# A two-layer graph network on one core: first routing spread over ScalarE and POOL, joined waves, slot operand in pieces, own room for first gathers

## The chip, the cores and the metric

The kernel runs on one core of a Trainium2 chip. The metric is the device time of one execution in microseconds; lower is better. The core has five engines that work side by side: TensorE (PE, with its weight loads as PEld), VectorE (DVE), ScalarE (ACT), GpSimd (POOL) and SyncE (SP), which here only issues DMA transfers. ScalarE and POOL issue transfers too.

## The reference

1250 nodes with 1024 features pass through two layers. Each layer adds a graph convolution and a linear attention to the rows, and then a mixture of experts. The change sits in the first layer's graph convolution and expert routing, and in the second layer's first steps:

```python
# L0_gnn: norm = dinv[src] * dinv[dst];  h = x @ W
out = segment_sum(h[src] * norm[:, None], dst) + b
x = x + relu(out) + L0_mix(xn)
# L0_ffn on layernorm(x), T = 1250, E = 8, K = 2
cap = int(1.25 * ((T * K + E - 1) // E))             # 391
probs = softmax(x @ router_gate)
topw, topi = top_k(probs, 2); topw = topw / (topw.sum(-1) + 1e-9)
gates[t, topi] = topw
top_g, tok_idx = top_k(gates.T, cap)                 # each expert keeps its 391 best tokens
xe = x[tok_idx]
h = silu(xe @ gate_w) * (xe @ up_w)
out.at[tok_idx].add((h @ down_w) * top_g)
# L1: x = x + sage(xn) + mix(xn), then x = x + ffn(layernorm(x))
```

## The kernel before

The rows are cut into ten tiles of up to 128 (`TS`, `TOK`). Work is written tile by tile; the framework that builds the kernel orders each engine's instructions at build time by its own estimate of when each is ready, so that an engine's order need not be that of the code. Each engine then works its list strictly in order. Tiles of memory come from pools with a fixed number of buffers; all PSUM results share eight banks (`bank`).

The first routing is one loop over tiles. In step `t`:

- the rows are loaded as `xt` (three buffers) in two halves on SP's queue (L691, L692);
- `gcn_rows` (L540) sums the neighbours into `pg` with 20 products (10 source tiles, each with a high and a low part; L497), scales and adds the bias on VectorE (`rgcn`, L544), and adds the relu to `xt` on VectorE (L546). The sum goes back to `res_d` (L694);
- `normalise` calls `layernorm` (L132): statistics on VectorE (L136, L138), the root on ScalarE (L140), the reciprocal and the final `(x - mean) * rs` on VectorE (L142, L143). The result `xn` is stored to `x1n_d` from ScalarE's queue (L598);
- `logits` of tile `t - 1` transposes `xn` (`pt`, eight 128x128 pieces, L607), copies it out as `xnt` with `evac` (which takes ScalarE and VectorE in turn, L115 and L117), and multiplies by the router (`plg`, 16 products, L612); `lg` is copied by VectorE (L613);
- at the end of a wave of tiles, `choose` takes the softmax (Exp on ScalarE, L621), the two best experts and their weights, some 22 small VectorE instructions.

Before, the waves are `[(0, 4), (4, 8), (8, 9), (9, 10)]`. One step after a wave is chosen, `turn_over` transposes its gates and choices (`ptg`, L646), and `rank` counts for every token how many tokens of its expert have a larger gate: a product `prow` (L666) brings the gates of a wave beside the tokens of a tile, and VectorE counts from PSUM (`junk`, L656 and L659). There are 80 such products over the four waves.

After the loop the counts are summed (`above`, L715), and places become a table of token numbers: `at_slot` (128x2560, one VectorE instruction, L727), `hit` and `what` (L730, L733), and 20 products `ptab` (L737), then `idx` and `idx_q`. For the first expert four indirect gathers on POOL (L775) bring rows into `xe`, which has two buffers; TensorE transposes them (`pte`, L781). Later experts gather quarters of rows into `xq` (L787). Each expert then runs `pgate`, `pup` (L809) and `py` (L821), some 63 us, and stores to `y_d` (L826).

The second layer begins with ten tiles of: load rows (`xt`, L877), gather two expert results (`yt`, L883, POOL), add them (L886), store, normalise, transpose, multiply. Ahead of it POOL clears `projT` and `kv` (L839, L843).

Of the kernel before, what the change touches and what calls it, by code (L numbers as in the profile page):

```python
# [10 lines left out]
F32 = mybir.dt.float32  # L11
F32R = mybir.dt.float32r
# [10 lines left out]
P = 128  # L23
# [3 lines left out]
T = 10  # L27
# [19 lines left out]
WAVES = [(0, 4), (4, 8), (8, 9), (9, 10)]  # L47
# [54 lines left out]
def network(tc: tile.TileContext, a: dict, out: bass.AP, env: SimpleNamespace, exact: bool):  # L102
# [29 lines left out]
    def layernorm(dst, x, ts):  # L132
# [9 lines left out]
        nc.vector.reciprocal(rs[:ts], sd[:ts])  # L142
        return nc.vector.tensor_scalar(dst, x, mv[:ts, 0:1], rs[:ts], op0=OP.subtract, op1=OP.mult)  # L143
# [396 lines left out]
    def gcn_rows(t, hn, b, x):  # L540
# [5 lines left out]
        nc.vector.scalar_tensor_tensor(x, r[:TS[t]], 0.0, x, op0=OP.max, op1=OP.add)  # L546
# [13 lines left out]
    with tc.tile_pool(name="route0a", bufs=1) as ra, tc.tile_pool(name="route0w", bufs=2) as rw:  # L560
# [31 lines left out]
        counted = {}  # L592

        def normalise(t, xt):
            ts = TS[t]
            xn = rw.tile([P, D], F32, name="xn1")
            layernorm(xn[:ts], xt[:ts], ts)
            nc.scalar.dma_start(x1n_d[TOK[t], :], xn[:ts])  # L598
            return xn

        def logits(t, xn):
            ts = TS[t]
            xnt = rw.tile([P, KB, P], F32, name="xnt")
            for b0 in (0, 4):
# [4 lines left out]
                evac(xnt[:, b0:b0 + 4, :ts], pt.rearrange("p (b q) -> p b q", b=4)[:, :, :ts])  # L609
# [3 lines left out]
            nc.vector.tensor_copy(lg[:ts, t, :], pl[:ts, :E])  # L613
# [27 lines left out]
        def turn_over(t0, t1):  # L641
            n = sum(TS[t0:t1])
            for src, dst in ((g2, gT), (oh2[:, 0], ohT[:, 0]), (oh2[:, 1], ohT[:, 1])):
# [3 lines left out]
                evac(dst[:, t0 * P:t0 * P + n], pt[:40, :n])  # L647
# [38 lines left out]

        ready, chosen = [], []
        for t in range(T + 1):
            if t < T:
# [3 lines left out]
                gcn_rows(t, hn, b, xt[:TS[t], 512:])  # L693
                nc.sync.dma_start(env.res_d[1][TOK[t], 512:], xt[:TS[t], 512:])  # L694
                ready.append(normalise(t, xt))
            if chosen:
                turn_over(*WAVES[chosen[0]])
                rank(chosen.pop())
            if t:
                logits(t - 1, ready[t - 1])  # L700
                for wave, (t0, t1) in enumerate(WAVES):
                    if t1 == t:
                        choose(t0, t1)
                        chosen.append(wave)
        turn_over(*WAVES[chosen[0]])
        rank(chosen.pop())
# [13 lines left out]
        for j in range(2, NG):  # L720
# [5 lines left out]
        at = tb.tile([P, T, 2, P], F32R, name="at_slot")  # L726
        nc.vector.tensor_tensor(at, slots.unsqueeze(1).unsqueeze(1).to_broadcast([P, T, 2, P]),  # L727
                                place.unsqueeze(3).to_broadcast([P, T, 2, P]), op=OP.is_equal)
# [4 lines left out]
        nc.vector.tensor_mul(what, hit, token.unsqueeze(3).to_broadcast([P, T, 2, E * NG]))  # L733
        pt = bank("ptab")
        for t in range(T):
            for k in range(2):
# [22 lines left out]
    s_table.close()  # L759
    loops(OP.subtract)  # L760
# [4 lines left out]
    with s_route:  # L765
        quarters = x1n_d.rearrange("n (j f) -> (n j) f", j=4)
        with tc.tile_pool(name="moe0", bufs=2) as mp:
            def columns(e):
                xeT = mp.tile([P, KB, ROWS], F32, name="xeT")
                if e == 0:  # L770

                    for g in range(NG):
                        n = min(P, SLOTS - g * P)
                        xe = mp.tile([P, D], F32, name="xe", bufs=2)
# [57 lines left out]

    s_x1 = ExitStack()
# [501 lines left out]
```

## Time and profile before

| | us |
|---|---|
| median of 3 runs | 3562.47 (3558.68 to 3562.52) |
| the profiled execution | 3579.93 |
| its span | 3578.2 |
| TensorE busy | 3381.7 |
| VectorE busy | 939.7 |
| POOL busy | 581.2 |
| ScalarE busy | 281.5 |
| mean granted TensorE clock | 0.966 |

The span runs from the first to the last instruction of one profiled execution. Busy time is summed by engine; TensorE's matmuls are pipelined, so that its busy time is no measure of work at full speed. PEclk is the share of full clock that TensorE was granted. A wait `A <- B: total, times, longest` says that A's engine was idle until B was done. In the timeline a row has start, duration, engine, line, operation, result and operands, and in brackets the idle time of the engine before it.

### The profile page before, as it was taken

What the parts mean: (1) busy time and instruction counts of PE and PEld (TensorE: products, weight loads), DVE (VectorE), ACT (ScalarE), POOL (GpSimd) and SP (SyncE); (2) the same over time, 40 slices, a digit from 0 to 9 for tenths busy, and PEclk for the clock granted to TensorE, in tenths of its full rate; (3) what the DMA queues carried; (4) which work ended last, traced back from release to release, by engine and by line L of the source; (5) the groups of instructions that cost most, each with busy time, mean ns of one, the idle gap of its engine ahead of it and who ended that gap; (6) DMA issues with size and microseconds to landing.
All of it is one profiled execution on the core that took longest, in us unless ns stands there. A gap on an engine that the chain in (4) does not pass through costs nothing.

```text
span 3578.2 us, 30558 instructions
## 1 busy us (share of the span) xinstructions
PE 3381.7 (95%) x12418; PEld 2119.7 (59%) x12418; DVE 939.7 (26%) x2482; ACT 281.5 (8%) x580; POOL 581.2 (16%) x493
## 2 busy tenths in 40 slices
PE   7999999999997689999789999999999999988997
PEld 3474756644655456767535465547777554557775
DVE  4257345621225512322160000011111111241111
ACT  1000011100001000000001011100000000001111
POOL 0016775051000231200020000010000000012221
PEclk9999999999998589999889999999999999988999
DMA  4724221062222143433460100120000110228884
GB/s 148 169 67 111 25 24 1 24 220 99 75 83 86 55 135 132 165 119 137 134 234 27 47 24 24 56 102 35 24 24 24 36 59 28 89 73 286 273 259 100
DMA packets 165010, 342.75 MB, mean 96 GB/s; under 512 B 37468, under 2 KB 58883, under 8 KB 162685
## 3 DMA queue, kind: packets, MB, share of 16 engines
q1 hardware_dynamic: 100204, 242.14, 20.0%
q0 software_dynamic: 39616, 52.68, 7.4%
q10 hardware_dynamic: 25040, 45.89, 3.8%
q8 instruction: 100, 1.64, 0.2%
q14 instruction: 50, 0.40, 0.0%
HBM read 261.79 MB, written 78.87 MB: 95 GB/s over the span
## 4 chain that ended last, share of the span: by engine, by line
PE 88%; DVE 5%; DMA 4%; issue 2%; ACT 1%; POOL 0%; SPq 0%; ACTq 0%; POOLq 0%; DVEq 0%
PE ph L158 8%; PE ppn L158 8%; PE pwo L158 8%; PE pqT L855 8%; PE pv L158 6%; PE pqk L158 6%; PE p L1265 5%; PE pa L497 5%; PE pgate L809 5%; PE pup L809 5%; PE py L821 5%; PE ph L996 4%; PE py L1276 2%; PE pg L497 2%; PE pkv L351 2%; PE po L399 2%
## 5 line engine op out<-in xcount | busy, mean ns | idle before, releaser
L259 POOL DMA_INDIRECT adj_d<-cnt,cell x167 | 259.3, 1552 | 90.0 <-issue 42.8
L1265 PE MATMUL p<-xeT,w 128*128 128x256 f32 (+1 forms) x1088 | 192.8, 338 | 4.8 <-ACT xeT L115 4.3
L809 PE MATMUL pgate<-xeT,wg 128*128 128x392 f32 x512 | 178.5, 500 | 10.6 <-issue 10.6
L1265 PEld LDWEIGHTS p<-xeT,w 128*128 128x128 f32 x1088 | 171.4, 191 | 24.8 <-ACT xeT L115 7.9
L809 PE MATMUL pup<-xeT,wu 128*128 128x392 f32 x512 | 176.3, 496 | 6.6 <-issue 6.6
L821 PE MATMUL py<-hT,wd 128*128 128x392 f32 x512 | 169.8, 492 | 0.0
L182 POOL TENSOR_TENSOR xr<-xr,bo 128x512 f32<-128x512 f32 (+1 forms) x40 | 50.4, 1264 | 714.3 <-PE pwo L158 453.8
L821 PEld LDWEIGHTS py<-hT,wd 128*128 128x128 f32 x512 | 160.5, 314 | 9.0
L158 PE MATMUL pqk<-wk,x0T 128*128 128x512 f32 (+1 forms) x320 | 145.3, 608 | 8.9 <-ACT x0T L115 7.5
L158 PE MATMUL pv<-wv,x1T 128*128 128x512 f32 (+1 forms) x320 | 144.2, 608 | 5.7 <-DVE x1T L117 3.4
L809 PEld LDWEIGHTS pgate<-xeT,wg 128*128 128x128 f32 x512 | 98.6, 193 | 82.7 <-issue 14.3
L809 PEld LDWEIGHTS pup<-xeT,wu 128*128 128x128 f32 x512 | 98.0, 191 | 81.2 <-issue 11.0
L158 PE MATMUL ph<-ws,h1T 128*128 128x512 f32 (+1 forms) x320 | 143.2, 596 | 0.0
L158 PE MATMUL pqk<-wq,x0T 128*128 128x512 f32 (+1 forms) x320 | 140.7, 593 | 0.0
L158 PE MATMUL ppn<-wn,x1T 128*128 128x256 f32 (+1 forms) x640 | 138.8, 379 | 0.0
L996 PE MATMUL ph<-x1T,ws 128*128 128x416 f32 (+1 forms) x384 | 138.2, 512 | 0.0
L158 PE MATMUL pv<-wv,x0T 128*128 128x512 f32 (+1 forms) x320 | 138.0, 592 | 0.0
L158 PE MATMUL ph<-wgcn,x0T 128*128 128x512 f32 (+1 forms) x320 | 138.0, 593 | 0.0
L158 PE MATMUL pwo<-wo,attn0T 128*128 128x512 f32 (+1 forms) x320 | 137.7, 592 | 0.1
L158 PE MATMUL ppn<-wn,h1T 128*128 128x512 f32 (+1 forms) x320 | 137.7, 592 | 0.0
L158 PE MATMUL pwo<-wo,attn1T 128*128 128x512 f32 (+1 forms) x320 | 137.5, 592 | 0.0
L855 PE MATMUL pqT<-x1T,wk 128*128 128x416 f32 (+1 forms) x384 | 135.6, 512 | 0.0
(369 smaller groups left out, 4460.2 us busy)
## 6 DMA issues: line engine op xcount, KB each, us to landing
w<-in_L_ffn_w_dram SPq DMA_DIRECT2D x17, 2048.0 KB
w<-in_L_ffn_w_dram SPq DMA_DIRECT2D x17, 1024.0 KB
wg<-in_L_ffn_gate_w_dram SPq DMA_DIRECT2D x8, 2048.0 KB
wu<-in_L_ffn_up_w_dram SPq DMA_DIRECT2D x8, 2048.0 KB
wd<-in_L_ffn_down_w_dram SPq DMA_DIRECT2D x8, 2048.0 KB
y_d<-ye ACTq DMA_DIRECT2D x30, 416.0 KB
adj_d<-ezero SPq DMA_DIRECT2D x2, 6105.0 KB
res_d<-xr SPq DMA_DIRECT2D x45, 256.0 KB
```

What stands on the lines that cost most here:

```text
L158: nc.tensor.matmul(pr[:TS[t], :cols], xT[:, k, TOK[t]], w[:, k, :], start=(k == 0), stop=(k == nk - 1))
L182: nc.gpsimd.tensor_add(xr[:TS[t]], xr[:TS[t]], bias[:TS[t]])
L259: nc.gpsimd.indirect_dma_start(out=adj_d[e % 2], out_offset=bass.IndirectOffsetOnAxis(ap=cell[:, e:e + 1], axis=0), in_=cnt[:, e:e + 1], i ...
L351: nc.tensor.matmul(pkv[f][:, :65], kf[:TS[t], i, f * P:(f + 1) * P], v[:TS[t], t, h, :], start=(t == 0), stop=(t == T - 1))
L399: nc.tensor.matmul(po[:TS[t], i, :], qf[:, hh, f, i * P:i * P + TS[t]], kv[:, h, f, :], start=(f == 0), stop=(f == 1))
L497: nc.tensor.matmul(pa, edges if by_node else feats, feats if by_node else edges, start=(s == 0 and i == 0), stop=(s == T - 1 and i == len( ...
L809: nc.tensor.matmul(pw[:, :SLOTS], w[:, k, ic], xeT[:, k, :SLOTS], start=(k == 0), stop=(k == KB - 1))
L821: nc.tensor.matmul(py[:, :SLOTS], wd[:, i, b::KB], hT[:, i, :], start=(i == 0), stop=(i == I0 // P - 1))
L855: nc.tensor.matmul(pq[:, :n], w[:, k, pair * P:(pair + 1) * P], xT[:, k, c0:c0 + n], start=(k == 0), stop=(k == KB - 1))
L996: nc.tensor.matmul(ps[:, :n], w[:, k, q0 + f * P:q0 + (f + 1) * P], xT[:, k, c0:c0 + n], start=(k == 0), stop=(k == KB - 1))
L1265: nc.tensor.matmul(pw_[:, :n], w12[:, k, off + i * P:off + (i + 1) * P], xeT[:, k, :n], start=(k == 0), stop=(k == KB - 1))
L1276: nc.tensor.matmul(py, hT[:, i, c * P:(c + 1) * P], w3[:, i, half * 512:(half + 1) * 512], start=(i == 0), stop=(i == H1 // P - 1))
```

## The change

It edits the routing loop, the table, the first expert's gathers and the placing of several pools:

- the last two waves become one, `(8, 10)`; `prow` products become 60;
- `rank` of a wave runs two tiles after its choice, behind the `logits` of that step;
- for all tiles but the last, the relu goes to ScalarE and the add to POOL (`gcn_rows`), and the last step of `layernorm` becomes two ScalarE passes and one small VectorE instruction;
- `xnt`, `lg` and the turned tables are copied by ScalarE alone; `x1n_d` is stored from SP's queue; an Exp on one column is placed behind the last norm;
- `at_slot` is made in five pieces of two tiles, after `hit` and `what`, between the `ptab` products;
- the first expert's four gathers have room of their own, in the two `xq` buffers;
- the second layer's `xt` rows get a pool of their own that is opened before the experts, its two clears move from POOL to VectorE, and `route1`, `pick1`, `x1T` and `h1T` are placed elsewhere (with `gw` loaded and `sc`, `so_far` cleared ahead of the second layer).

```diff
-WAVES = [(0, 4), (4, 8), (8, 9), (9, 10)]
+WAVES = [(0, 4), (4, 8), (8, 10)]
...
-    def layernorm(dst, x, ts):
+    def layernorm(dst, x, ts, last_on_act=False):
...
+        if last_on_act:
+            mm = small.tile([P, 1], F32, name="mm")
+            nc.vector.tensor_scalar(mm[:ts], mv[:ts, 0:1], -1.0, None, op0=OP.mult)
+            nc.scalar.activation(dst, x, AF.Identity, bias=mm[:ts])
+            return nc.scalar.activation(dst, dst, AF.Copy, scale=rs[:ts])
         return nc.vector.tensor_scalar(dst, x, mv[:ts, 0:1], rs[:ts], op0=OP.subtract, op1=OP.mult)
...
-    def gcn_rows(t, hn, b, x):
+    def gcn_rows(t, hn, b, x, spread=False):
...
-        nc.vector.scalar_tensor_tensor(x, r[:TS[t]], 0.0, x, op0=OP.max, op1=OP.add)
+        if spread:
+            nc.scalar.activation(r[:TS[t]], r[:TS[t]], AF.Relu)
+            nc.gpsimd.tensor_add(x, r[:TS[t]], x)
+        else:
+            nc.vector.scalar_tensor_tensor(x, r[:TS[t]], 0.0, x, op0=OP.max, op1=OP.add)
...
-            layernorm(xn[:ts], xt[:ts], ts)
-            nc.scalar.dma_start(x1n_d[TOK[t], :], xn[:ts])
+            layernorm(xn[:ts], xt[:ts], ts, last_on_act=t < T - 1)
+            if t == T - 1:
+
+                tc.keep_in_program_order(nc.scalar.activation(power, eps_t, AF.Exp))
+            nc.sync.dma_start(x1n_d[TOK[t], :], xn[:ts])
...
-                evac(xnt[:, b0:b0 + 4, :ts], pt.rearrange("p (b q) -> p b q", b=4)[:, :, :ts])
+                nc.scalar.copy(xnt[:, b0:b0 + 4, :ts], pt.rearrange("p (b q) -> p b q", b=4)[:, :, :ts])
...
-            nc.vector.tensor_copy(lg[:ts, t, :], pl[:ts, :E])
+            nc.scalar.copy(lg[:ts, t, :], pl[:ts, :E])
...
-                evac(dst[:, t0 * P:t0 * P + n], pt[:40, :n])
+                nc.scalar.copy(dst[:, t0 * P:t0 * P + n], pt[:40, :n])
...
-        for t in range(T + 1):
+        for t in range(T + 2):
...
-                gcn_rows(t, hn, b, xt[:TS[t], 512:])
+                gcn_rows(t, hn, b, xt[:TS[t], 512:], spread=t < T - 1)
...
-            if chosen:
-                turn_over(*WAVES[chosen[0]])
-                rank(chosen.pop())
-            if t:
+            if 0 < t <= T:
                 logits(t - 1, ready[t - 1])
...
-                        chosen.append(wave)
-        turn_over(*WAVES[chosen[0]])
-        rank(chosen.pop())
+                        chosen.append((wave, t))
+            while chosen and (chosen[0][1] < t - 1 or t == T + 1):
+                wave = chosen.pop(0)[0]
+                turn_over(*WAVES[wave])
+                rank(wave)
...
-        at = tb.tile([P, T, 2, P], F32R, name="at_slot")
-        nc.vector.tensor_tensor(at, slots.unsqueeze(1).unsqueeze(1).to_broadcast([P, T, 2, P]),
-                                place.unsqueeze(3).to_broadcast([P, T, 2, P]), op=OP.is_equal)
...
+        at = tb.tile([P, T, 2, P], F32R, name="at_slot")
         pt = bank("ptab")
         for t in range(T):
+            if t % 2 == 0:
+                nc.vector.tensor_tensor(at[:, t:t + 2], slots.unsqueeze(1).unsqueeze(1).to_broadcast([P, 2, 2, P]),
+                                        place[:, t:t + 2].unsqueeze(3).to_broadcast([P, 2, 2, P]), op=OP.is_equal)
...
     s_table.close()
+
+    s_rows = ExitStack()
+    rows1 = s_rows.enter_context(tc.tile_pool(name="rows1", bufs=3, side="right"))
     loops(OP.subtract)
...
+                    room = [mp.tile([P, NI, B, KB], F32, name="xq").rearrange("p i c b -> p (i c b)") for _ in range(2)]
...
-                        xe = mp.tile([P, D], F32, name="xe", bufs=2)
+                        xe = room[g // 3][:, g % 3 * D:(g % 3 + 1) * D]
...
-    xT = s_x1.enter_context(tc.tile_pool(name="x1T", bufs=1, side="right")).tile([P, KB, N], F32, name="x1T")
+    xT = s_x1.enter_context(tc.tile_pool(name="x1T", bufs=1)).tile([P, KB, N], F32, name="x1T")
...
-        nc.gpsimd.memset(projT, 0.0)
+        nc.vector.memset(projT, 0.0)
...
-        nc.gpsimd.memset(kv, 0.0)
+        nc.vector.memset(kv, 0.0)
...
-                    lnp = s_ln.enter_context(tc.tile_pool(name="ln1", bufs=3))
+                    lnp = s_ln.enter_context(tc.tile_pool(name="ln1", bufs=2))
...
-                        xt = lnp.tile([P, D], F32, name="xt2")
+                        xt = rows1.tile([P, D], F32, name="xt2")
...
-                            yt = lnp.tile([P, D], F32, name=f"yt{k}", bufs=2)
+                            yt = lnp.tile([P, D], F32, name=f"yt{k}")
...
-    h1T = s_sage.enter_context(tc.tile_pool(name="h1T", bufs=1)).tile([P, KB, N], F32, name="h1T")
+    h1T = s_sage.enter_context(tc.tile_pool(name="h1T", bufs=1, side="right")).tile([P, KB, N], F32, name="h1T")
```

The allocations of `route1` and `pick1`, with the `gw` load and the clears of `sc` and `so_far`, move unchanged from behind the second layer's attention to ahead of `x1T`.

## The prediction

> **What bounds the kernel now.** I read the page's busy shares first, then the chain of waits to find where TensorE is not on it, then the stages there by windows, waits and timeline.
>
> ```profile
> PE 3381.7 (95%) x12418; PEld 2119.7 (59%) x12418; DVE 939.7 (26%) x2482; ACT 281.5 (8%) x580; POOL 581.2 (16%) x493
> ```
>
> TensorE bounds the kernel as a whole, so only stretches where it idles can be won. The change touches two: the first routing (1042 to 1236.5 us) and the hand-over from the first experts to the second layer (1766.9 to 1799.1).
>
> ```profile
> core 0: us, PE busy (x) PEld busy (x) DVE busy (x) ACT busy (x) POOL busy (x), PEclk, DMA share, GB/s
> 1062.00:1087.00 25.00, 23.89 (x138) 19.99 (x137) 13.71 (x30) 3.79 (x7) 1.29 (x3) 1.00 0.49 170
> 1087.00:1112.00 25.00, 10.67 (x47) 8.29 (x47) 17.21 (x84) 3.68 (x7) 0.68 (x4) 0.72 0.25 91
> 1145.10:1205.30 60.20, 39.95 (x139) 28.50 (x138) 50.07 (x256) 5.68 (x11) 2.79 (x14) 0.56 0.03 11
> 1205.30:1236.50 31.20, 12.37 (x57) 10.96 (x57) 11.42 (x26) 2.08 (x5) 13.44 (x14) 0.55 0.35 106
> 1766.90:1799.10 32.20, 0.00 (x0) 0.00 (x0) 7.28 (x12) 1.78 (x3) 7.66 (x8) 0.55 0.72 232
> ```
>
> See the four kinds: a TensorE-bound tile loop; a hole at the first wave; a tail where VectorE (50 of 60 us) sets the pace at half clock; and two stretches where table, gathers and loads follow each other. Two waits name the hole:
>
> ```profile
> PE ptg L646 <- DVE g L636: 19.2, 4, 7.7
> PE plg L612 <- DVE xnt L117: 12.5, 6, 6.3
> ```
>
> **The loop and the hole (gain 8).** The loop's period is 8.0 us (rgcn at 1063.4, 1071.3, 1079.4): pg 20 x 0.23 = 4.7, pt 1.04, plg 1.95, small gaps. From the end of pg of tile 5 (1087.0) to the start of tile 6's (1111.1) are 24.1 us, of which TensorE's own work (12 ptg at 0.24, 8 prow at 0.28, pt and plg 3.0) is 8.2: 15.9 us are wait. First for the choice (ptg 7.7), then because the xnt copy sits on VectorE behind 8.4 us of counts (6.3) and tile 6's pg behind that plg. The change ranks wave 0 two tiles later, when the choice is long done, and copies xnt, lg and the turned tables on ScalarE. What is late next: 8 prow products want the 8 PSUM banks, freed at about 1 us each by the counts; and the choice still swaps ScalarE's table twice (1.28 each) ahead of one norm (ACT_TABLE_LOAD, 1283 ns). I leave 4 us of wait, between 0 and 8: 12 saved.
>
> Against it stands a longer chain to xn. It loses the 0.69 (L546) and the 0.81 (L143) on VectorE and gets a relu on ScalarE, an add on POOL, a small VectorE instruction (0.16) and two ScalarE passes of 1024. The groups have the nearest rows:
>
> ```profile
> L182 POOL TENSOR_TENSOR xr<-xr,bo 128x512 f32<-128x512 f32 (+1 forms) x40 | 50.4, 1264 | 714.3 <-PE pwo L158 453.8
> ...
> L278 ACT ACTIVATE sq<-q 128x512 f32<-128x512 f32 x36 | 22.7, 631 | 117.4 <-DVE q L276 102.5 <-DVE dup L252 8.8 <-DVE off L256 3.2
> ```
>
> Relu 0.63 and add 1.26 for 0.69; two passes of 1.07 (0.63 plus 512 more elements at (0.597 - 0.272)/384 = 0.85 ns, from L908's kf of 512 and 128) for 0.81: with the small one and four hand-overs of 0.05, about 3 us more per tile for tiles 0 to 8. VectorE gives back 2.4 us of queue per tile (0.69, 0.81, the 0.68 xnt copy, the 0.17 lg). Before, the chain from pg to xn took 6.6 us (1063.2 to 1069.9) and pt came 1.2 us later; bare it would be 3.8, so 2.8 were queueing. So it becomes 6.8 to 9.6, against the 7.7 to 8.0 that TensorE has of other work: mostly covered. If that cover is gone, the cost is up to 1.6 us x 8 tiles = 13.
>
> The GPSIMD Engine Reference of the Trainium skill (4.1 Engine selection) speaks against this: elementwise work belongs on VectorE, GpSimd being about 2x slower with two inputs. The rows agree on the price (1264 against 691 ns). By the rule the swap loses (0.63 + 1.26 - 0.69) x 9 = 11 us and the total falls to 24; by the rows most lies under the next pg, and the rule says nothing of that. I follow the rows. The skill's SBUF page (Who interferes with whom) adds that a VectorE and a GpSimd instruction can lock each other out; no row here shows it (POOL's adj, L489, takes 0.41 to 0.46 beside a busy VectorE). Bounds: 0 to one 0.75 instruction a tile, 7 us; I take 0 and keep 7 for the range.
>
> Both xnt copies in one queue also run plg in one piece. Before, tiles 6 to 8 did so, and their pg ran part of its way at 0.43 instead of 0.23 us a product (6.3 against 4.9 us): a period of 9.7. I charge 1 us to each of four tiles: 4. Net 12 - 4 = 8, between -5 and 14. The x1n_d stores move from ScalarE's queue to SP's: ten issues of 0.35 us. Each waits there for its Copy, and behind it queue the next res_d store and the xt loads, for which an add three tiles on waits. Those loads need the same tile's buffer back and have two periods (16 us) to land, which took 3.5 to 5.4 in the chain: 0, and 3 if that cover goes.
>
> **The tail (gain 15).** From the end of the last pg (1145.1) to the sum of the counts (1205.3): 8.3 to the first count of wave 1, 19.1 of counts, 7.7 of plg, choice and ptg, 8.0 of counts, 8.6 of the same again, 8.6 of counts. By width a count steps at 0.68 (512), 0.54 (384), 0.41 (256), 0.27 (128 and the mask), 0.24 (98). Joined, wave 2 has per choice 8 + 1 counts of 226 (0.37, interpolated), 4 of 512, one of 128, one of 98, two masks: 7.1, twice 14.1, against 16.6. More important, one choice chain is gone and the other lies beside wave 1's counts. After: 6 to the first count (choose of wave 1 starts before the last pg), 19.1, choose 4.2 on VectorE itself, 14.1, and 1.6 of in-order waits: 45. If wave 1's ranks truly waited for the last choice, as the code reads, it would be 12 + 33 = 45 too. Gain 15, between 10 and 19. The Exp preload, queued behind the last root on ScalarE, moves a 1.28 table load ahead of the last choice; the xnt copies of tile 8 can queue behind it, for which plg of tile 8 waits: between -1.5 and 1.5, taken as 0.
>
> **Table and first gathers (gain 7.4).** From the timeline:
>
> ```profile
> 1206.68 2.82 DVE L727 TENSOR_TENSOR at_slot<-slots,place 128x2560 fp32r<-128x2560 f32 x1
> ...
> 1211.36 4.45 PE L737 MATMUL ptab<-what,at_slot 128*128 128x32 f32 x20 [8.36 <-DVE what L733]
> ...
> 1219.01 1.04 POOL L775 DMA_INDIRECT xe<-x1n_d,idx  x1 [24.38 <-issue]
> ...
> 1227.91 0.95 POOL L775 DMA_INDIRECT xe<-x1n_d,idx  x1 [0.30 <-PE pte L781]
> ...
> 1236.49 7.91 PE L809 MATMUL pgate<-xeT,wg 128*128 128x392 f32 x16
> ```
>
> In pieces, only a fifth of at_slot (0.6) stands ahead of ptab; TensorE (0.89 per two tiles) then runs slower than VectorE (0.6): 2.4 saved. The third gather waited for a buffer until 1227.9 with expert 1's gathers let past it; with own room four issues at 1.26 end at 1224, land about 5 us later, and pte (1.95 a tile) ends near 1230.5: 6 less. But the layer-2 rows (xt, 3 x 0.5 MB) leave the second experts' memory too and can now load right then, on an SP queue that has nothing to issue until 1298; at 230 GB/s they cost up to 6, I take 1: gain 5, between 0 and 6. Expert 1's 13 gathers (1.26 each) now wait for the room of the first ones: they start near 1230 instead of 1221 and are done by 1252, with pgate of expert 1 at 1299 for cover.
>
> **Hand-over (gain 4).** From the chain of waits between y_d's landing and the second layer's first rows:
>
> ```profile
> 1778.36 0.95 POOL proj L839
> 1779.31 1.03 POOL kv L843
> 1780.50 0.95 POOL yt L883
> 1781.76 9.53 DMA yt<-y_d,slot_of
> ```
>
> The two memsets (0.95 and 1.03) stand on the chain, and the gather came 2.1 us after the first began; on VectorE, which idles until 1789.8 waiting for xt, they cost nothing: 2.1. The 1.5 MB of xt beside the yt gathers is gone: of 9.5 us I take 2 off. Between 1.5 and 5.5. The moved route1, pick1, x1T and h1T pools free no wait: at 2433 and 2801 us TensorE runs on but for 1.5 us of pmrow. I take 0, plus or minus 2, for them, and 0 for the gw load (one issue of 0.4 on SP, now ahead of bqT, P and bv: the gathers on POOL do not wait for these).
>
> **Sum.** 8 + 15 + 7.4 + 4 = 34.4 from the profiled execution's 3579.9, which lies 17 us above the median; the same microseconds come off the median: 3562.5 - 34.4 = 3528. A measurement of this kernel tells about 0.2% (7 us) from no change.
>
> **Rivals.** (a) *The longer chain shows* (16%): xn comes 2 us late per tile, 8 x 2 = 16, gain 18: 3544. For it: ScalarE now carries 4.4 us per 8 us period (relu 0.63, root 0.29, passes 2.1, copies 1.2, lg 0.2), in order. Against: VectorE, 13.7 of 25 us busy, gets 2.4 us freer in each tile. (b) *Slower* (8%): on ScalarE the xnt copies of tile t-1 queue behind the norm of tile t, as the code is written. Then plg waits for rgcn, relu, add, norm: a period of 4.7 + 7 + 1.2 + 2 = 15 against 8, in 8 tiles 56 lost; the hole's 12 and the other 26 are still won: +18, 3580. It decides from 38/8 = 4.8 us a tile on, a period of 12.8. Against it, ScalarE's order in the trace is not the code's:
>
> ```profile
> 1072.02 0.58 ACT L115 COPY xnt<-pt 128x512 f32<-128x512 f32 x1 [3.29 <-DVE rgcn L544]
> ...
> 1075.89 0.29 ACT L140 ACTIVATE sd<-mv,eps_t 128x1 f32<-128x1 f32 x1 [3.29 <-DVE mv L138]
> ```
>
> The copy of tile 2 came ahead of the root of tile 3, which stands first in the code: order goes by readiness. (c) *No change* (6%): loads of early rows, bank waits and (a) eat the gain: 3560. (d) As forecast: 70%, 3514 to 3541.
>
> **How the numbers follow.** Likeliest 3528. The range leaves out (b), (c) and the far ends: 3511 to 3551. Faster 0.86 (a and d), same 0.06, slower 0.08.
>
> **What would show it.** Right: no hole over 5 us between pg of tiles 5 and 7; loop period 8 to 9.5; prow 60 instead of 80; last pg to the sum of counts about 45; ptab about 3.6 us after that sum; four xe issues in a row; yt gathers 0.3 us after y_d lands. Wrong: pt waiting for ACT xn in most tiles, xnt copies after the norm of the next tile, the last pg later than 1145, or xe gathers landing beside xt loads.

## The result, and the profile after

The changed kernel takes 3523.76 us (median of 4 runs, 3522.38 to 3524.27), the kernel before 3560.71 beside it: a ratio of 0.9896, 95% interval 0.9879 to 0.9913. That is 37 us faster, between 31 and 43, where 34.4 were predicted. The profiled execution of the changed kernel has a span of 3520.6 us, that of before 3578.2. These two differ by 57.6 us, 21 more than the medians: the profile of before carries some 24 us that, as e1 to e5 show, belong to neither kernel.

The busy shares on the page of the changed kernel:

```profile
PE 3369.1 (96%) x12398; PEld 2112.8 (60%) x12398; DVE 914.0 (26%) x2398; ACT 314.3 (9%) x630; POOL 592.3 (17%) x496
```

TensorE is busy for 12.6 us less. Of these, 7.3 are in the first experts (513.2 to 505.9), where the work is the same and the profile of before has the stretch that e1 looks at, and 3.3 are in the tail, which has 20 prow products fewer. The rest of the gain is idle time. Its windows, which answer to the five stretches shown of before (loop, first wave, tail, table and gathers, hand-over):

```profile
core 0: us, PE busy (x) PEld busy (x) DVE busy (x) ACT busy (x) POOL busy (x), PEclk, DMA share, GB/s
1062.00:1087.00 25.00, 24.29 (x133) 20.40 (x132) 8.26 (x20) 10.93 (x20) 5.07 (x6) 0.93 0.54 179
1087.00:1112.00 25.00, 23.23 (x133) 18.57 (x131) 15.96 (x83) 16.13 (x25) 4.47 (x9) 1.00 0.41 143
1135.10:1183.40 48.30, 36.66 (x119) 23.52 (x117) 40.42 (x188) 8.31 (x17) 2.63 (x10) 0.56 0.04 13
1183.40:1207.60 24.20, 10.63 (x56) 10.32 (x56) 9.52 (x28) 2.05 (x5) 4.48 (x5) 0.54 0.41 153
1713.50:1742.50 29.00, 1.79 (x8) 1.57 (x8) 9.91 (x15) 2.37 (x4) 6.14 (x7) 0.57 0.75 205
```

In the second row TensorE works 23.2 of 25 us, where it worked 10.7: the hole at the first wave is gone. VectorE is still busy there (16.0 us, most of them counts), but TensorE waits for none of it in this stretch. The tail is 48.3 us instead of 60.2, table and gathers 24.2 instead of 31.2. From the last py to the first pv of the second layer, the last row, it is 29.0 us instead of 34.0; the row shown of before ends 1.8 us ahead of its first pv. The waits of TensorE over loop and tail have changed hands (columns: us in total, times, longest):

```profile
PE pt L620 <- ACT xn L147: 7.8, 3, 3.9
PE prow L679 <- DVE junk L672: 3.0, 7, 0.5
PE pt L620 <- DVE xn L148: 2.9, 1, 2.9
PE plg L625 <- ACT xnt L622: 2.7, 9, 0.8
```

The two that named the hole (19.2 for the choice, 12.5 for the copy xnt on VectorE) are gone or small; in their place pt waits for the normalised row on ScalarE, three times. Where the hole was, the timeline of the changed kernel now reads:

```profile
1098.63 0.39 PE L502 MATMUL pg<-hn_lo,adj 98*128 98x512 f32 x1
1098.85 1.07 PE L620 MATMUL pt<-ident,xn 128*128 128x128 f32 x8
1100.17 1.06 PE L625 MATMUL plg<-rg,xnt 128*128 128x8 f32 x8 [0.24 <-ACT xnt L622]
1101.08 0.60 PE L659 MATMUL ptg<-ident,g 128*40 128x128 f32 x4
...
1103.64 2.13 PE L679 MATMUL prow<-gT,ohT 40*128 40x512 f32 x8 [0.28 <-ACT ohT L660]
1105.70 0.50 PE L502 MATMUL pg<-hn_hi,adj 128*128 128x512 f32 x1
```

From the last pg of tile 6 to the first of tile 7 are 6.7 us, of which 0.5 are wait; before it was 24.1 us between tiles 5 and 6, of which 15.9 were.

To compare the experiments below, every profile was cut into six stages at the same events, read from its timeline: first pg to last pg (loop), last pg to the sum of counts (tail), to ptab (table), to the first pgate (gathers), to the last py (experts), and to the first pqT behind the ten tiles of the second layer (hand-over). In us:

| profile | loop | tail | table | gathers | experts | hand-over |
|---|---|---|---|---|---|---|
| before | 103.4 | 60.1 | 6.0 | 25.1 | 530.4 | 122.6 |
| after | 94.1 | 48.1 | 4.8 | 19.4 | 505.9 | 117.6 |
| e1 before again | 103.5 | 60.1 | 6.0 | 24.8 | 532.1 | 122.4 |
| e2 rank at once | 103.6 | 51.7 | 4.8 | 20.2 | 530.0 | 115.0 |
| e3 norm on VectorE | 94.9 | 48.1 | 4.8 | 20.6 | 529.7 | 117.3 |
| e4 four waves | 100.8 | 50.6 | 4.8 | 19.6 | 530.5 | 117.0 |
| e5 after again | 95.6 | 48.1 | 4.8 | 21.0 | 505.8 | 114.6 |
| e6 wave 1 early | 97.7 | 42.7 | 4.8 | 20.7 | 505.9 | 114.7 |
| e7 table and rows | 94.9 | 48.1 | 3.9 | 18.9 | 505.8 | 114.0 |
| e8 gathers paced | 100.1 | 48.1 | 4.8 | 19.3 | 505.8 | 117.6 |
| e9 hand-over undone | 95.3 | 48.1 | 4.8 | 19.2 | 505.8 | 120.6 |
| e10 logits two behind | 98.8 | 48.1 | 4.8 | 20.9 | 505.9 | 117.3 |
| e11 all orders | 97.8 | 44.0 | 3.9 | 19.5 | 505.9 | 114.5 |
| e12 three orders | 95.0 | 42.7 | 3.9 | 19.6 | 507.5 | 114.3 |

The experiments ran on four chips. On two of them the kernel before takes 3558 to 3560 us, on the other two (e1 to e4 on one, e12 on the other) 3583 to 3584; ratios are always to the kernel before on the same chip. Most of the stages repeat within 1 us in profiles that share their instructions; the loop (94.1 to 100.8), the gathers (19.3 to 21.0) and the hand-over (114.0 to 117.6) do not.

### The profile page after: what moved, and what is told of

Read it like the earlier page. It is cut to its first block, busy times and chain, and to the rows that moved or that the text cites. A ratio compares the mean times of both kernels' runs of the same rounds, so it can differ in the third digit from the quotient of the medians.

```text
span 3520.6 us, 30464 instructions
## 1 busy us (share of the span) xinstructions
PE 3369.1 (96%) x12398; PEld 2112.8 (60%) x12398; DVE 914.0 (26%) x2398; ACT 314.3 (9%) x630; POOL 592.3 (17%) x496
## 3 DMA queue, kind: packets, MB, share of 16 engines
q1 hardware_dynamic: 101612, 247.26, 20.9%
## 4 chain that ended last, share of the span: by engine, by line
PE 89%; DVE 4%; DMA 3%; ACT 1%; issue 1%; POOL 0%; SPq 0%; POOLq 0%; ACTq 0%; DVEq 0%
PE ph L163 8%; PE ppn L163 8%; PE pwo L163 8%; PE pqT L891 8%; PE pv L163 7%; PE pqk L163 6%; PE p L1284 5%; PE pa L502 5%; PE pgate L827 5%; PE py L839 5%; PE pup L827 5%; PE ph L1015 4%; PE py L1295 3%; PE pg L502 2%; PE pkv L356 2%; PE po L404 2%
```

## Experiments

**e1: the kernel before, profiled again.** No edit.

> The kernel before, unchanged, profiled once more. In the first profile of it TensorE did single products 1.3 to 2.7 us apart from 1249.7 to 1277 us (10.12 us busy of 27.3) with no releaser but issue, in expert 0, a part of the program that the change hardly touches; there the two profiles differ by 24.5 us (531.7 against 507.1 from the first pgate to the last y_d store), which the prediction has no term for. Theory A: this hole belongs to that one execution, which was 17 to 19 us above the others (3579.9 against 3559 to 3563): the new profile has no such hole, first pgate to y_d store takes 507 to 510 us, and the time is 3558 to 3563. Theory B: the hole is there in every execution of the kernel before: 530 us again in that stretch; then the change gained 24 us there and only about 13 in the routing and the hand-over, and the terms of the prediction are far too large.

Measured: 3584.27 us, beside 3583.97 for its own copies (ratio 0.9999, 0.999 to 1.0007). Theory A is wrong as written, since the hole is there again; its windows in the new profile:

```profile
1235.40:1248.70 13.30, 13.30 (x34) 7.56 (x35) 4.77 (x4) 1.19 (x1) 9.95 (x12) 0.81 0.36 104
1248.70:1276.20 27.50, 10.38 (x21) 4.28 (x19) 0.00 (x0) 0.50 (x1) 18.07 (x19) 0.66 0.32 95
1276.20:1300.00 23.80, 23.80 (x65) 13.20 (x65) 1.69 (x3) 1.49 (x3) 0.00 (x0) 0.89 0.06 11
```

TensorE works 10.4 of 27.5 us, and POOL issues gathers all that time. But theory B is wrong too: e2 to e4, variants of the changed kernel that ran on the same chip, have the same 530 us of experts, and the kernel before takes 24 us more there than in the first runs. The hole comes with the chip or its state, not with the kernel. The profile of before that the prediction was read from has this hole, and lies 17 us above its median; by their level (3559 to 3563) the timed runs had none.

**e2: rank a wave one tile after its choice again.**

```diff
+            while chosen and chosen[0][1] < t:
+                wave = chosen.pop(0)[0]
+                turn_over(*WAVES[wave])
+                rank(wave)
             if 0 < t <= T:
                 logits(t - 1, ready[t - 1])
...
-            while chosen and (chosen[0][1] < t - 1 or t == T + 1):
-                wave = chosen.pop(0)[0]
-                turn_over(*WAVES[wave])
-                rank(wave)
```

> The changed kernel with one part undone: a wave is turned over and ranked one tile after its choice, ahead of that tile's logits, as in the kernel before; everything else stays. Theory (the prediction's hole): the wait for the choice and then the plg behind the counts come back: about 12 us between pg of tiles 5 and 6, last pg at 1147 instead of 1135.1, and since wave 1 is ranked one step sooner too, its counts start a few us earlier in the tail (3 to 5 given back): 3523.8 + 12 - 4 = 3532. Rival 1: the freed VectorE and the ScalarE copies had closed the hole by themselves, and the later place is worth under 3 us: 3520 to 3526. Rival 2: the earlier start of wave 1's counts is worth more than the hole costs: under 3520.

Measured: 3557.71, ratio 0.9923 (0.9909 to 0.9936), against 0.9896 for the whole change. The loop is back at 103.6, 9.5 above the changed kernel's 94.1, and at the first wave TensorE waits for the choice again:

```profile
1097.28 1.04 PE L659 MATMUL ptg<-ident,g 128*40 128x128 f32 x4 [5.52 <-DVE g L649]
1098.12 1.91 PE L659 MATMUL ptg<-ident,oh 128*40 128x128 f32 x8
1100.51 3.78 PE L679 MATMUL prow<-gT,ohT 40*128 40x512 f32 x8 [0.48 <-ACT ohT L660]
1104.22 1.97 PE L620 MATMUL pt<-ident,xn 128*128 128x128 f32 x8
1106.01 3.58 PE L625 MATMUL plg<-rg,xnt 128*128 128x8 f32 x16
```

Of the two waits of the hole only the first is back (5.5 us; 7.7 before). The second, 6.3 us of plg behind the counts, is not: the copies on ScalarE took that one away. What follows the wait runs at half clock (pt 1.97 instead of 1.04). The tail did not get shorter, as both theory and the second rival had it, but longer, 51.7 for 48.1. Wave 1's counts do start sooner (9.1 us behind the last pg instead of 13.5), but all of wave 1's products now stand ahead of the logits of tiles 8 and 9, and VectorE idles 3.4 and 1.9 us for the last choice and its tables.

**e3: relu, add and norm back on VectorE.**

```diff
-            layernorm(xn[:ts], xt[:ts], ts, last_on_act=t < T - 1)
+            layernorm(xn[:ts], xt[:ts], ts)
...
-                gcn_rows(t, hn, b, xt[:TS[t], 512:], spread=t < T - 1)
+                gcn_rows(t, hn, b, xt[:TS[t], 512:])
```

> The changed kernel with the relu, the add and the last step of the norm of tiles 0 to 8 back on VectorE (two instructions of 0.69 and 0.81 us a tile for relu 0.63, add 1.28, two passes of 1.15 and the small 0.15); the copies stay on ScalarE, the ranks two tiles behind. Theory (the prediction): the longer chain to xn lies under the next pg and VectorE has room, so the time is the same within 4 us: 3520 to 3528. Rival (a) of the prediction: the longer chain shows, and without it every tile is about 2 us faster: last pg at about 1120, time 3508. Rival (c): the relief of VectorE is what closes the loop; with 1.4 us more of it a tile, and wave 0's counts beside it, the loop gets about 1 us a tile longer: 3532.

Measured: 3546.96 beside 3583.97, ratio 0.9893 (0.9878 to 0.9908), the same as the whole change; loop 94.9, tail 48.1. By the time the theory holds: this part of the change is worth nothing measurable either way, and VectorE did not need the relief once copies and ranks were moved. But the profile shows that the longer chain is not free. The loop of e3, and under it that of the changed kernel (columns as in the windows above):

```profile
1041.70:1136.60 94.90, 86.64 (x416) 70.73 (x415) 51.62 (x173) 18.82 (x42) 6.03 (x21) 0.86 0.46 152
1041.20:1135.30 94.10, 83.62 (x416) 67.99 (x415) 39.42 (x160) 43.51 (x69) 16.83 (x26) 0.89 0.45 153
```

TensorE idles 8.3 us in the first and 10.5 in the second, and 10.4 to 11.5 in all eight profiles that have the changed kernel's loop as it is (after, e4 to e9, e12). What e3 gains there goes into slow products: 46 of its 200 pg products ran at half rate, against 30 (e4 says more of these), some 3 us. Why they were more is not shown. So the longer chain costs the loop 2 to 4 us, as an estimate from this one profile, and the time can't tell that from nothing.

**e4: four waves again.**

```diff
-WAVES = [(0, 4), (4, 8), (8, 10)]
+WAVES = [(0, 4), (4, 8), (8, 9), (9, 10)]
```

> The changed kernel with the last two tiles in waves of their own again (four waves, 80 prow products instead of 60); everything else stays. Theory (the prediction): the tail gets the narrower counts (33.2 instead of 28.2 us for the two choices' waves of tiles 8 and 9, 2 x 16.6 against 2 x 14.1 as costed, or at least 2.5 for one of them) and a second chain of choice and ptg, of which half lies beside counts: last pg to the sum of counts 55 instead of 48.3, time 3530.5. Rival: the counts are all that matters and both choices hide beside wave 1's counts: 2.5 us, 3526. Rival: wave 8 can start sooner than the joined one and nothing changes: 3524.

Measured: 3552.31, ratio 0.9913 (0.9899 to 0.9926), 6 us above the whole change. But the tail gives only 2.5 of it (50.6), the first rival's number: the second choice hides beside wave 1's counts. In this profile VectorE waits for no choice once wave 1's counts have begun. The other 6 us of this profile are in the loop (100.8), whose instructions are in the same order on TensorE, VectorE, ScalarE and POOL as in the changed kernel. There the rate of the products differs:

```profile
1078.83 0.95 PE L625 MATMUL plg<-rg,xnt 128*128 128x8 f32 x8
1079.63 0.53 PE L502 MATMUL pg<-hn_hi,adj 128*128 128x512 f32 x1
1079.96 0.63 PE L502 MATMUL pg<-hn_lo,adj 128*128 128x512 f32 x1
1080.39 0.63 PE L502 MATMUL pg<-hn_hi,adj 128*128 128x512 f32 x1
```

A product of 0.39 us takes 0.63, a step of 0.43 instead of 0.23, though TensorE's last wait of more than 0.24 us ended at 1056. Of the loop's 200 pg products 30 were that slow in after, e5, e7 and e9 (loops of 94.1 to 95.6), 43 in e6 (97.7), 52 and 53 in e8 and e4 (100.1 and 100.8): 23 more times 0.2 us are 4.6 of the 6. A loop is only comparable to within these 6 us. The five timed runs lie apart in the same way, two near 3558 (this profile is one of them) and three near 3551.5.

**e5: the changed kernel again.** No edit.

> The changed kernel, unchanged, beside the kernel before on the same chip. The first batch showed, in the kernel before and in three variants of the changed one alike, a TensorE hole of 23 to 24 us in expert 0 (10.12 us of work in 27.3) that the first profile of the changed kernel does not have. Theory A: the hole belongs to the chip or its state and not to either kernel: where the kernel before is at 3584 this one shows the hole too and is at 3547 (ratio 0.9896 as before); where the kernel before is at 3560 neither has it and this one is at 3524. Theory B: the change removes the hole: 3524 beside 3584, ratio 0.983.

Measured: 3526.08 beside 3558.42, ratio 0.9911 (0.9897 to 0.9924). On this chip neither kernel is raised; the experts take 505.8, without a hole. Theory A, though only half of it was tried: the changed kernel itself was not run on a chip where the kernel before is at 3584, only its variants e2 to e4.

**e6: wave 1 earlier in the tail.**

```diff
+            if t == T:
+                turn_over(*WAVES[1])
+                rank(1, (0,))
             if 0 < t <= T:
                 logits(t - 1, ready[t - 1])
...
+            if t == T:
+                rank(1, (1,))
```

> The changed kernel with wave 1 turned over, and ranked for the first choice of each token, ahead of the logits of the last tile, and for the second choice behind the last choice; waves 0 and 2 stay. In the changed kernel the first count of wave 1 starts 13.7 us after the last pg, behind the last tile's norm and logits, although the choice of wave 1 is done at 1138.9, 3.7 us after it. Theory (it is the order of the tables behind the last plg that the tail lost against the predicted 6 us): counts start 4 to 8 us earlier, and last pg to the sum of counts is 41 to 44 instead of 48.3: 4 to 8 us faster than the changed kernel. Rival: the last tile's logits now wait behind twelve prow products for PSUM banks, the last choice comes late and VectorE idles for it ahead of wave 2's counts: same or up to 5 us slower.

Measured: 3518.49, ratio 0.9889 (0.9874 to 0.9904); beside e5 on the same chip 7.6 us less, of which the tail gives 5.4: it is 42.7 instead of 48.1. The first choices of wave 1 are ranked ahead of the last logits, the second ones behind the last choice. VectorE's first count of wave 1 in the timeline of the changed kernel:

```profile
1148.78 0.75 DVE L669 TENSOR_SCALAR_CACHE_REDUCE junk<-prow,wts 128x512 bf16<-128x512 f32 x1 [0.65 <-PE prow L679]
```

And in this one:

```profile
1146.39 0.75 DVE L669 TENSOR_SCALAR_CACHE_REDUCE junk<-prow,wts 128x512 bf16<-128x512 f32 x1 [1.53 <-PE prow L679]
```

The last pg ended at 1135.3 and 1138.9: the count starts 13.5 us behind it in the one, 7.5 in the other. So the tail was late because the turned tables stood behind the last tile's norm and plg on TensorE and ScalarE. With the ranks split in two, VectorE never waits again behind this first count, while e2 lost 5.3 us to the last choice.

**e7: at_slot behind what, early rows behind the gathers.**

```diff
+                with tc.issue_after(what_ins.ins):     # pieces two to five
                     nc.vector.tensor_tensor(at[:, t:t + 2], ...
...
+                        with tc.issue_after(late.ins): # late: expert 1's loads of wg and wu
                             last_rows = nc.sync.dma_start(xt[:ts], env.res_d[1][TOK[t], :])
```

> The changed kernel with two small orders changed: the second to fifth piece of at_slot behind what, and the three early loads of second-layer rows (xt2) behind the first loads of expert 1's weights on SP's queue, so that they do not land beside the first gathers. Theory (these are the two missing pieces of the predicted 2.4 and the reason why the first gather took 6.6 us to be used against 4.5): sum of counts to ptab 3.6 instead of 4.84, ptab to first pgate 17.4 instead of 19.4: 3.2 us faster than the changed kernel. Rival: ptab is bound by the pieces either way and the gathers share the DMA engines only with each other: ptab to pgate the same 19.4, and at most 1 us in all.

Measured: 3523.94, ratio 0.9909 (0.9893 to 0.9924): 2 us less than e5, which the interval doesn't tell from nothing. By stages, table 3.9 instead of 4.8 (one of five pieces, not three, ahead of what), gathers 18.9, the lowest of all. Early rows in the way:

```profile
1194.29 1.29 SPq L913 DMA_DIRECT2D xt<-res_d  x3
```

This line is of the changed kernel, 1.6 us ahead of its first gather, and its first pte came 6.6 us after that gather (7.1 in e5). Without these loads it came after 4.6, here and in e9, and after 4.5 in the kernel before. But the last gather ends the stage, so that of 2 to 2.5 us only 0.5 to 2 reach pgate.

**e8: the next expert's gathers paced.**

```diff
+                    after_hT = nc.gpsimd.tensor_copy(probe, hT[:, 0, 0:1])   # of the running expert
+                    with tc.issue_after(after_hT.ins):
                         for i in range(NI):
                             nc.gpsimd.indirect_dma_start(out=xq[:, i] ...
```

> The changed kernel with the 13 quarter gathers of the next expert held on POOL until the first block of hT of the running expert is there (a copy of 128x1 on POOL reads it), so that no more than 13 gathers follow each other, where 39 in a row (49 us) are issued in the profiles. Theory (the hole is TensorE without instructions while POOL issues gathers without a break; in the profiles with it, it begins some 28 us into the row and ends within 3 us of its last gather): on a chip that shows it the hole goes, first pgate to last y_d store 507 instead of 531, and the kernel is 24 us faster than the changed one there (about 3523 beside 3547); on a chip without it, no difference. Rival: the hole is tied to expert 0 itself (weights, code) and not to the gathers: still there, same time. Rival: the gathers now come late for DVE's transposes and expert 1 to 7 wait: slower by 7 x a few us.

Measured: 3525.04, ratio 0.9904 (0.9889 to 0.992), as e5. This chip has no hole, so the theory was not tried; the second rival is out, since holding the gathers back costs TensorE nothing (505.8).

**e9: the hand-over undone.**

```diff
-                        xt = rows1.tile([P, D], F32, name="xt2")
+                        xt = lnp.tile([P, D], F32, name="xt2", bufs=3)
...
-        nc.vector.memset(projT, 0.0)
+        nc.gpsimd.memset(projT, 0.0)
...
-        nc.vector.memset(kv, 0.0)
+        nc.gpsimd.memset(kv, 0.0)
```

> The changed kernel with the hand-over to the second layer undone: its rows (xt2) in the second layer's own buffers again, so that they load only when the experts' memory is free, beside the yt gathers, and the two memsets back on POOL ahead of the gathers. In the profiles the last py to the first pv takes 34.0 us before and 29.0 to 29.4 after, and to the first pqT, behind all ten tiles, 122.5 before and 114 to 117.6 after. Theory (these two edits are the hand-over's gain, predicted 4, by the profiles 5 to 8): last py to first pv 34, to pqT 120 to 123: 5 to 7 us slower than the changed kernel (3530 beside 3558, or 3553 beside 3584). Rival: the moved pools (route1, pick1, x1T) made the gain and the ten-tile loop is bound by its transfers anyway: at most 2 us slower.

Measured: 3529.14 beside 3560.23, ratio 0.9918 (0.9905 to 0.9932); the hand-over takes 120.6, the last py to the first pv 33.6 instead of 29.0. The theory holds by the stage; in the time, the interval does not part it from e5 (0.9911). Its timeline:

```profile
1726.25 0.95 POOL L875 MEMSET proj<- 128x1024 f32 x1 [261.21 <-DMA y_d<-ye]
1727.14 0.95 POOL L879 MEMSET kv<- 128x1024 f32 x1
1728.25 0.96 POOL L919 DMA_INDIRECT yt<-y_d,slot_of  x1 [0.15 <-issue]
...
1736.96 1.28 DVE L922 SCALAR_TENSOR_TENSOR xt<-yt,wts,xt 128x1024 f32<-128x1024 f32 x1 [10.60 <-DMA xt<-res_d]
```

The memsets are 2.0 us of it, and then the first sum waits for the row xt, not for yt. In the changed kernel that sum starts 4.7 us after the first gather's issue, here 8.7.

**e10: logits of the first tiles two behind.**

```diff
                 gcn_rows(t, hn, b, xt[:TS[t], 512:], spread=t < T - 1)
+                if 2 <= t <= 6:
+                    logits(t - 2, ready[t - 2])
+                    if t == 5:
+                        choose(*WAVES[0])
+                    if t == 6:
+                        turn_over(*WAVES[0])
+                        rank(0)
...
```

> The changed kernel with the logits of tiles 0 to 4 two tiles behind pg instead of one (from tile 5 on as before), the choice of wave 0 a tile later and its ranks in the same place. In the changed kernel pt of tile 0 waits 3.07 us for xn, and the next pg then runs 8.5 us at 0.43 instead of 0.23 us a product, 4 us in all. Theory (the wait for xn is what is left of the predicted loop, and the slow products follow it): no wait ahead of the first pt, pg of tiles 1 to 5 at 0.23, and first to last pg 88 to 90 us instead of 94 to 100: 5 to 8 us faster. Rival: the slow products come whether TensorE has waited or not, only elsewhere: 3 us. Rival: the choice of wave 0 now comes too late for its ranks and the hole is back at tile 6: slower by 3 to 8.

Measured: 3527.23 beside 3560.23, ratio 0.9903 (0.9887 to 0.9918): no gain, loop 98.8. Both rivals have a share. TensorE idles 8.6 us in the loop, 2 to 3 less than in the changed kernel's, but 48 pg products were slow, 18 more than its 30 and 3.6 us. The first wait is still there, under another name, for ScalarE's copies of tile 0 (1061.13) stand behind the norm of tile 1 and the relu of tile 2 (1058.1 to 1061.2):

```profile
1061.75 1.87 PE L625 MATMUL plg<-rg,xnt 128*128 128x8 f32 x8 [4.91 <-ACT xnt L622]
```

And pg of tile 7 follows that of tile 6 after 16 us instead of 6.7 (1098.5 to 1114.5), with ranks, pt and plg of two tiles between them, mostly at half rate.

**e11: all four orders.** The edits of e6, e7, e8 and e10 together.

> The changed kernel with the four orders together: logits of tiles 0 to 4 two behind, wave 1 early in the tail, at_slot and the early rows later, gathers paced. Theory: the stages are in series, so the gains add up: about 6 (loop) + 5.4 (tail, as measured: 48.1 to 42.7) + 1 to 2 (table and gathers) = 12 to 14 us below the changed kernel, 3512 beside 3558; and where the kernel before is at 3584 with the hole in expert 0, the paced gathers take that away as well: 3512 there too, instead of 3536. Rival: the hole stays whatever the gathers do: 3536 beside 3584. Rival: a gain in one stage is lost in the next (a later choice of wave 0, a colder clock): 3518 or more beside 3558.

Measured: 3519.07 beside 3560.23, ratio 0.9889 (0.9874 to 0.9904), no better than e6 alone. Beside e6's stages, table and gathers are 2.1 us shorter, the tail is 1.3 longer (44.0) and the loop no shorter (97.8). The last rival.

**e12: three orders.** The edits of e6, e7 and e8.

> The changed kernel with the three orders that did what they were meant for: wave 1 early in the tail (tail 48.1 to 42.7), at_slot and the early rows later (table 4.84 to 3.89; first gather used after 4.6 instead of 6.6 to 7.1 us), and the gathers paced; the logits one tile behind pg as in the changed kernel, since two behind brought the hole at wave 0 back (pg of tile 6 to pg of tile 7: 22 to 23 us against 13.6). Theory: 5.4 + 1 + 1 us, and nothing lost elsewhere: 7 us below the changed kernel, 3518 beside 3559, with a loop of 94 to 101 us by the number of slow pg products; and where the kernel before is at 3584, no hole: about 3518 there as well. Rival: no better than the early wave 1 alone (ratio 0.9889), because the first transposes only start sooner and the last gather ends them: 3519 to 3520; and the hole stays where there is one.

Measured: 3520.38 beside 3583.25, ratio 0.9826 (0.9812 to 0.9839). This chip is one of the two where the kernel before is 24 us slower, and here these have come off: the experts take 507.5, and in the stretch of the hole TensorE does not stop, while POOL is busy for 12.6 us with its 13 gathers and then rests:

```profile
1202.70:1238.00 35.30, 35.30 (x103) 20.25 (x103) 8.34 (x8) 2.62 (x4) 12.60 (x14) 0.95 0.17 49
1238.00:1266.00 28.00, 28.00 (x86) 23.55 (x85) 7.34 (x15) 0.50 (x1) 0.00 (x0) 1.00 0.54 206
```

For the changed kernel itself this chip's time was not measured; by the ratio of the first result it would be near 3546 here (3583.25 x 0.9896). So the three orders are worth about 26 us on such a chip, by this estimate; on the others these three were not run without e10's, and e6 alone gives 7.6 there. There is no profile of this chip without the pacing: that its 24 us are the same hole is read from the time, and that the pacing took it away and not the other two edits is argued from where the hole lies.

## Why the prediction was right

The time (3523.8 for 3528) and the likeliest case were right. The medians gain 37.0 us here and 32.3 on e5's chip, for 34.4. By stages the changed kernel gains 9.3 + 12.0 + 1.2 + 5.7 + 5.0 = 33.2 us (e5: 7.8 + 12.0 + 1.2 + 4.1 + 8.0 = 33.1). The gains are in the places forecast, but the terms miss by up to 4 us each, to both sides, so that the sum is nearer than its terms; that part is luck.

- *Loop and hole (8 predicted, 7.8 to 9.3 measured).* The stretch is 17.4 us shorter (24.1 to 6.7), where 12 were taken: the late ranks took the wait for the choice, and the copies on ScalarE that of plg, as e2 shows. But the loop is only 7.8 to 9.3 shorter, so some 8 to 10 us came back, where 4 were charged. First, pt of tile 7 waits 3.9 us for its norm. On VectorE rgcn of tile 7 starts 2.0 us after its pg, behind wave 0's counts, and the end of its statistics (mv) stands behind rgcn of tile 8:

```profile
1116.33 0.69 DVE L136 BATCH_NORM_STATS2 st<-xt 128x6 f32<-128x512 f32 x1 [2.37 <-POOL xt L553]
1118.47 0.75 DVE L549 SCALAR_TENSOR_TENSOR rgcn<-pg,dinv,bgcn 128x512 f32<-128x512 f32 x1 [1.45 <-PE pg L502]
1119.14 0.20 DVE L138 BATCH_NORM_AGGREGATE mv<-st 128x2 f32<-128x12 f32 x1
...
1122.35 1.09 PE L620 MATMUL pt<-ident,xn 128*128 128x128 f32 x8 [3.91 <-ACT xn L147]
```

  Second, pg of tile 9, behind that wait and parted by a plg, takes 9.3 us at mostly half rate. Third, the first pt waits 3.1 instead of 2.0. What was charged for, 1 us a tile for plg in one piece, did not show: plg still ran in two pieces, and tiles 3 to 6 took 8.1 us each (8.0 before). Two terms were wrong in size, and they cancelled: that the 8 came out is luck.
- *The longer chain (0 taken, up to 13 feared) and POOL's add.* Each pass took 1.15 us (1.07 estimated), the relu 0.63, the add 1.27 to 1.28 beside a busy VectorE, so no lock-out shows. By e3's time the chain costs nothing that can be told, by its profile 2 to 4 us of loop, so that the 0 was too low and most of the chain was covered all the same. The rule of the Trainium skill's GPSIMD Engine Reference (4.1 Engine selection), that elementwise work belongs on VectorE, is right on the price of an instruction and here on the direction as well; the 11 us that the prediction worked out from it did not come, for what is covered. Rival (b) did not come up: no copy stood behind a norm for long in the changed kernel (longest wait 0.8); it took e10's order to bring a wait of that kind (4.9 us).
- *Tail (15 predicted, 12.0 measured).* The mis-sized term is "6 to the first count": it was 13.5. The counts were as costed (34.6 us from first count to sum for 37.4; wave 2 14.2 for 14.1). Two table loads of 1.28 each lie in the 13.5 us (1138.55 for the root, 1140.16 for the preload, which the prediction took as 0). e6 has them too and starts at 7.5, so the 6 us between the two are the order and not the preload. In e6, though, ScalarE copies the turned tables only behind the preload, and TensorE waits 1.7 us for that copy. Joining the waves is 2.5 of the 12 (e4), less than the prediction gave it.
- *Table and gathers (2.4 + 5 predicted, 1.2 + 4.1 to 5.7 measured).* Only a fifth of at_slot was to stand ahead of ptab; three of five pieces do (e7 gives back 0.9). Four gathers issue in a row as forecast. The early rows cost the first gather 2 to 2.5 us and the stage less, for the 1 us taken; gathers landing beside xt loads was one of the signs named for being wrong, and it came up at this small size.
- *Hand-over (4 predicted, 5.0 to 8.0 measured).* Right in both parts (e9), and a bit small: from the first gather to the first sum it is 4.7 us for 9.3, where 2 us were taken for the gathers' transfer, since that sum had waited for the row xt and now waits for yt. Before and after:

```profile
1789.78 1.28 DVE L886 SCALAR_TENSOR_TENSOR xt<-yt,wts,xt 128x1024 f32<-128x1024 f32 x1 [10.32 <-DMA xt<-res_d]
1729.89 1.28 DVE L922 SCALAR_TENSOR_TENSOR xt<-yt,wts,xt 128x1024 f32<-128x1024 f32 x1 [2.96 <-DMA yt<-y_d,slot_of]
```

- *What the prediction missed.* In the profile of before, TensorE idles 17 us between 1249.7 and 1277, in the stretch right behind the last one examined. It was no part of the change, so the forecast was not hurt; but "the same microseconds come off the median" was said of a profile with 24 us in it that the median doesn't have. Had the change shortened that stretch, the sum would have been wrong by that much.

## What to carry to other kernels

A wait at a hand-over between engines is won by ordering: where the ranks stand decided 9.5 us of the loop (e2) and 5.4 of the tail (e6), while moving three elementwise steps to idle engines gained nothing and made a chain longer (e3). When the ordering is loosened, look at once at what stands behind the moved work on the in-order engine, since the next wait was there each time (tile 7's norm, the last tile's tables, e10's copy). And when a profile lies well above the median of the timed runs, find where before adding up gains against it.

## What the runs showed of the hardware

In five profiles TensorE stalled while POOL issued gathers without a break; on other chips it did not. Windows of e3, with 39 gathers, one each 1.26 us, from 1209.5 to 1258.3:

```profile
1210.00:1230.00 20.00, 20.00 (x63) 11.63 (x63) 7.26 (x6) 2.28 (x3) 15.13 (x17) 1.00 0.33 98
1230.00:1238.00 8.00, 8.00 (x25) 4.54 (x24) 0.00 (x0) 0.00 (x0) 6.17 (x7) 1.00 0.38 107
1238.00:1260.00 22.00, 6.38 (x10) 2.10 (x8) 0.00 (x0) 0.00 (x0) 15.48 (x17) 0.62 0.35 105
```

And its timeline, three of the products in the third row:

```profile
1247.40 0.81 PE L827 MATMUL pup<-xeT,wu 128*128 128x392 f32 x1 [1.99 <-issue]
1250.20 0.81 PE L827 MATMUL pup<-xeT,wu 128*128 128x392 f32 x1 [1.99 <-issue]
1253.00 0.81 PE L827 MATMUL pup<-xeT,wu 128*128 128x392 f32 x1 [1.99 <-issue]
```

Most of the products come one each 2.80 us, with no releaser in the profile, from 28 us after the first of these gathers until 3 us after the last; in before and e1 TensorE idles in the same way from 1249 to 1277. In before and in e1 to e4 the first idle time of over 0.9 us comes 27 to 34 us after the row of gathers began, but 16 to 29 us after the first pgate: the stall goes with the gathers rather than with a place in the expert. Elsewhere the same row of gathers (1207 to 1255 in after) leaves TensorE at 24.0 of 24.0 us, and the experts take 505.8 to 505.9 in after and e5 to e11. With 13 gathers in a row (e12) it is absent on a chip where the kernel before takes 3583 us, which is one profile. That TensorE lacked instructions is a reading of "issue", not shown; why the chips differ stays open.

The other: the half-rate stretches of TensorE (0.43 instead of 0.23 us a product, 30 to 53 of 200 products) often follow a wait of 3 us or more, but e4's from 1079.6 on does not, and in one and the same order of instructions the loop moved by 6 us with their number.
